# A graph layer on one Trainium2 core: the nodes' own half moves to the middle stage, the permutation gets its own PSUM tile, the order of issue is new

## Chip, core and metric

The kernel runs on one core of a Trainium2 chip. The core has four engines that work in order, each on its own queue: PE (TensorE, matmuls into PSUM), DVE (VectorE), ACT (ScalarE) and POOL (GpSimd). SP (SyncE) issues DMAs. The metric is the device time of one execution in microseconds; the time before is 4208.68 us, the median of 3 runs (4205.73 to 4212.73).

## What is computed

12,500 nodes with 256 features, 200,000 edges (src, dst, weight) sorted by dst. Two graph layers, each added to its input and normalised over the 256 features:

```
feat      = relu(x @ W[o] + b)                       o = 0: self, 1: neighbour; 4 heads of 32
edge_w    = (leaky(att . self)[src] + leaky(att . nei)[dst]) * weight
agg[src] += edge_w * feat_nei[dst]
per head, for self and agg:  (f - mean) * scale * rsqrt(var + 1e-9) + offset
x1  = layernorm(x + concat(self, agg))
msg = relu(concat(x1[src], x1[dst]) @ W_msg + b_msg);   s[dst] += msg
out = layernorm(x1 + layernorm_affine(relu(concat(x1, s) @ W_upd + b_upd)))
```

What the change is about is the self half of the first layer: for each node 128 values (4 heads of 32), centred, divided by the root of their variance, scaled, and added with the offset to the node's x.

## The kernel before

It has three stages.

**First stage, 0 to about 1262 us.** It goes over 112 groups of 14 x 128 edges. In each group it projects 128 nodes twice: the window xw, in which the group's dst values lie (neighbour half), and block xb, the g-th block of 128 nodes (self half, for the 98 groups that have a block). The steps of one group are small functions. `transposes`, `keep`, `project` and `relu` give the features R; `att_mult` and `att_sum` the attention; `mean_sum` and `centre` the centred features F; `part0` to `part3` split the neighbour half into three bf16 parts. The self half then goes through `square` (ACT), `var` (DVE), `root` (ACT), `rstd`, `norm`, `scale` and `put` (DVE) into y, which begins as x plus offset (`offsets`, DVE), and `out_y` stores y in the DRAM table yd.

The edges of a group are sorted by the block of src with one-hot matmuls: `hot` and `hot_b` (DVE) make one-hots, `ranks` (PE) counts, `quarter` (ACT) and `rows` (DVE) round, `begins` (PE), `keep_begins` and `keep_v` (ACT) give the places, `shift` and `reach` (DVE), `steps` (PE), `steps_keep` (ACT), `steps_low` (DVE), `target` (PE) and `index` (DVE) the rows in the log; `place_mm0` to 2 (PE) and `pick0` to 13 (ACT, L667) find each edge's slot; `split`, `hot_r`, `hot_q` and `goods` (DVE) build the operands of `permute` (PE, L696), which puts the edges into order. `extras` (DVE) and `rel_keep` (ACT) read its result. `rel_turn`, `rel_row`, `rel_out` and `rel_in` send the edges' places in the window through DRAM (reld), so that they come back as a row on all partitions (rr); `hot_n` (DVE, L724) compares it; `message0` to 5 (PE, L733) and `evict0` to 5 (ACT, L740) build the messages, and `scatter0` to 3 (POOL, L746) write them into a log in DRAM by indirect DMA.

PSUM tiles of this stage: "fs" (2 of them) is one bank per group; it holds the counts and places, the projection's result and, behind them, the permutation's result. "mp" (3) holds messages, "wp" (2) places, "tp" (1) transposes.

The order of issue is written out by hand: the table AT gives each step a number, step number plus 256 times the group is its place, and all steps of all groups are issued in that order (PE, ACT, DVE and SP keep it exactly). Numbers above 256 mean that a step runs beside the first steps of later groups. Every eighth group the m_ steps (transposes, casts, pair counts) prepare the edge data of eight groups.

**Middle stage, 1262 to 2180 us.** For each of the 98 blocks of nodes the log is read back in five parts: `log_load` (SP), `log_hot` (products by POOL for four parts, by DVE for the fifth; one-hots by DVE, L957), `log_sum` (PE, L965). For batches of up to four blocks (27 batches) `heads_a` to `heads_d` normalise the summed half, `load_y` fetches y from yd, and `stats`, `root`, `rstd`, `offset` and `store_x1` make x1; `proj_t` to `proj_s` project x1 for the second layer. The list `work` is ordered by step, five steps to a block.

**Last stage, 2180 us to the end.** Second layer: gathers by POOL, messages and sums. It is not touched.

Of the kernel before, what the change touches and what calls it, by code (L numbers as in the profile page):

```python
# [11 lines left out]
def _warn_once_fixed(msg, *args, **kwargs):  # L12
# [6 lines left out]
FT = mybir.dt.float32  # L19
# [3 lines left out]
AF = mybir.ActivationFunctionType  # L23
OP = mybir.AluOpType
AX = mybir.AxisListType

P = 128
# [13 lines left out]
    "widen": -271, "hot": -174, "hot_b": -168, "ranks": 42, "quarter": 50, "rows": 89, "begins": 127,  # L41
    "keep_begins": 141, "keep_v": 143, "shift": 201, "reach": 177, "steps": 278, "steps_keep": 303,
# [3 lines left out]
    "split": 381, "hot_r": 405, "goods": 453, "hot_q": 408, "permute": 455, "rel_keep": 503, "extras": 529,  # L46
    "rel_turn": 547, "rel_row": 566, "rel_out": 625, "rel_in": 741, "hot_n": 778, "message0": 830,
# [3 lines left out]
    "project": 180, "relu": 228, "offsets": 376, "att_mult": 309, "mean_sum": 308, "att_sum": 362,  # L51
    "centre": 331, "leaky_n": 392, "part0": 401, "part1": 420, "part2": 561, "part3": 772, "leaky_s": 528,
    "square": 358, "var": 661, "root": 691, "rstd": 725, "norm": 824, "scale": 861, "put": 978, "out_y": 1060,
    "m_load": -1480, "m_cast0": -1441, "m_cast1": -1438, "m_col0": -1038, "m_keep0": -1037, "m_col1": -599,
    "m_keep1": -542, "m_col2": -871, "m_keep2": -834, "m_block": -970, "m_place": -904, "m_high": -277,
    "m_rest": -229, "m_mid": -167, "m_low": -92, "m_win": -504, "m_turn": -771, "m_pairs": -755, "m_mask": -727,
    "m_count": -420,
# [45 lines left out]
def kernel(  # L103
# [45 lines left out]
    yd = dram.tile([ROWS, D], FT, name="yd")  # L149
# [68 lines left out]
    with ExitStack() as l0:  # L218
# [210 lines left out]
        def feat_tasks(g):  # L429
# [28 lines left out]
            def offsets():  # L458
                st["y"] = feat.tile([P, D], FT, name="y", bufs=3)
                nc.vector.tensor_tensor(st["y"], xb[g], ofb, op=OP.add)  # L460

# [58 lines left out]
            def square():  # L520
                st["q"] = feat.tile([P, HD], FT, name="q")
                nc.scalar.activation(st["q"], st["F"][:, 0:HD], AF.Square)

            def var():
                st["v"] = feat.tile([P, H], FT, name="v")
                nc.vector.tensor_reduce(st["v"], st["q"].rearrange("p (h k) -> p h k", h=H), AX.X, OP.add)

            def root():
                nc.scalar.activation(st["v"], st["v"], AF.Sqrt, bias=epsh, scale=1.0 / 32)

            def rstd():
                nc.vector.reciprocal(st["v"], st["v"])

            def norm():
                c = st["F"][:, 0:HD].rearrange("p (h k) -> p h k", h=H)
                nc.vector.tensor_tensor(c, c, st["v"][:, :, None].to_broadcast([P, H, 32]), op=OP.mult)

            def scale():
                c = st["F"][:, 0:HD]
                nc.vector.tensor_tensor(c, c, scb[:, 0:HD], op=OP.mult)  # L540

            def put():
                nc.vector.tensor_tensor(st["y"][:, 0:HD], st["y"][:, 0:HD], st["F"][:, 0:HD], op=OP.add)

            def out_y():
                nc.sync.dma_start(yd[g * P:(g + 1) * P, :], st["y"])
# [3 lines left out]
            return dict(transposes=transposes, keep=keep, project=project, relu=relu, offsets=k(offsets),  # L550
                        att_mult=att_mult, mean_sum=mean_sum, att_sum=att_sum, centre=centre, leaky_n=w(leaky_n),
                        part0=w(part(0)), part1=w(part(1)), part2=w(part(2)), part3=w(part(3)),
                        leaky_s=k(leaky_s), square=k(square), var=k(var), root=k(root), rstd=k(rstd),
                        norm=k(norm), scale=k(scale), put=k(put), out_y=k(out_y))
# [13 lines left out]
        def sort_tasks(g):  # L568
# [124 lines left out]
            def permute():  # L693
                mv = st["mv"].rearrange("p t r m -> p t (r m)")
                for t in range(GT):
                    nc.tensor.matmul(st["sm"][:, 16:16 + 5 * NR], st["qh"][:, :, t], mv[:, t],  # L696
                                     start=(t == 0), stop=(t == GT - 1))
                st["go"] = st["sm"][:, 16:16 + 5 * NR].rearrange("p (r m) -> p r m", m=5)
# [212 lines left out]
    with ExitStack() as bar:  # L911
# [704 lines left out]
```

## Time and profile before

| | us |
|---|---|
| median of 3 runs | 4208.68 |
| the profiled execution | 4196.61 |
| its span, first to last instruction | 4194.8 |
| first stage | about 1262 |
| middle stage | about 918 |
| last stage | about 2015 |

The page gives busy times for each engine over the span; "PEld" is PE's weight load, which overlaps its matmuls. "PEclk" is the clock that the throttle granted PE, 1.00 being full. Rows of groups read: line, engine, operation, output from inputs, shapes, count, then busy us and mean ns of one, then the engine's idle time before them with what ended it. Rows of waits read: who waited, for whom, us in total, times, the longest. Rows of a stretch read: from, to and length in us, then the busy time and instruction count of PE, PEld, DVE, ACT and POOL, the granted clock, the DMA engines' busy share and GB/s. Rows of the timeline read: start and length in us, engine, line, operation, how many, and in brackets the idle time ahead with its cause. Records of neighbouring instructions on one engine overlap a little, so that their mean lengths add up to more than the busy time.

### The profile page before, as it was taken

The page shows a single profiled execution, that of the slowest core. Times are in us where ns is not written, and L with a number is a line of the kernel's source. Part 1 is how long each engine was busy: PE and PEld are TensorE (multiplying, and loading weights), DVE is VectorE, ACT ScalarE, POOL GpSimd, SP SyncE. Part 2 cuts the span into 40 slices and gives each one's busy share as a digit, 9 for nine tenths or more (in the row PEclk, how much of TensorE's full clock was granted, in tenths as well). Part 3 has the DMA queues.
Part 4 walks back from the last instruction along what each step waited for, and adds up shares of the span by engine and source line. Part 5 has one row for each costly group of instructions (what it writes and reads, how often), then busy time and mean ns, then how long its engine had stood idle before and what let it go on. Part 6 is the DMA issues. An engine that isn't in the chain of part 4 may idle for free.

```text
span 4194.8 us, 86344 instructions
## 1 busy us (share of the span) xinstructions
PE 3623.5 (86%) x26432; PEld 3058.0 (73%) x26432; DVE 3206.7 (76%) x9815; ACT 2478.4 (59%) x8632; POOL 2616.8 (62%) x2461
## 2 busy tenths in 40 slices
PE   7889899998889999999988878878888787888876
PEld 6778787777778888888876666666666666666665
DVE  8988989899868888888876666667666666666665
ACT  6998889999881222222235555556565555555555
POOL 2555545555455555555537777777777777777775
PEclk9999999999999999999999999999999999999999
DMA  4776765555556666666656666666666666666664
GB/s 156 242 242 231 237 208 197 191 190 193 173 189 194 185 186 184 181 184 183 187 156 170 171 170 169 170 170 171 171 171 171 172 171 168 172 171 170 171 171 128
DMA packets 457247, 763.84 MB, mean 182 GB/s; under 512 B 75772, under 2 KB 300574, under 8 KB 456782
## 3 DMA queue, kind: packets, MB, share of 16 engines
q1 hardware_dynamic: 326622, 415.17, 34.2%
q0 software_dynamic: 110848, 327.87, 25.6%
q10 hardware_dynamic: 19312, 15.21, 1.1%
q8 instruction: 216, 3.54, 0.4%
q14 instruction: 249, 2.04, 0.2%
HBM read 553.43 MB, written 204.54 MB: 181 GB/s over the span
## 4 chain that ended last, share of the span: by engine, by line
PE 45%; DMA 22%; DVE 16%; ACT 7%; issue 5%; POOL 4%; DVEq 0%; SPq 0%; ACTq 0%; POOLq 0%
PE sum L965 19%; DMA gb<-pd,srcf 19%; PE agg L1363 6%; POOL gb L1285 4%; DVE gb L1344 4%; PE mp L733 4%; ACT gb L1346 3%; PE qp L1322 2%; PE qm L1053 2%; DMA rr<-reld 2%; PE fs L696 2%; PE fs L600 1%; PE fs L467 1%; DMA reld<-rT 1%; DVE oT L724 1%
## 5 line engine op out<-in xcount | busy, mean ns | idle before, releaser
L1285 POOL DMA_INDIRECT gb<-pd,srcf x1563 | 1507.9, 965 | 511.8 <-issue 283.2
L1363 PE MATMUL agg<-gb,o 128*128 128x256 f32 x3126 | 866.9, 400 | 263.8 <-ACT gb L1346 259.2
L1344 DVE TENSOR_TENSOR gb<-qp,gb 128x512 f32<-128x512 f32 x781 | 538.9, 690 | 653.1 <-DMA gb<-pd,srcf 466.7
L746 POOL DMA_INDIRECT log<-m,ix x448 | 631.4, 1409 | 621.8 <-ACT rT L708 264.4
L1346 ACT ACTIVATE gb<-gb 128x512 f32<-128x512 f32 x781 | 491.3, 629 | 790.4 <-DVE gb L1344 786.8
L1363 PEld LDWEIGHTS agg<-gb,o 128*128 128x128 f32 x3126 | 557.0, 192 | 493.5 <-ACT gb L1346 434.3
L965 PE MATMUL sum<-lg,o 128*128 128x256 f32 x3724 | 836.8, 378 | 11.2 <-DMA lg<-log 11.2
L965 PEld LDWEIGHTS sum<-lg,o 128*128 128x128 f32 x3724 | 696.3, 189 | 108.9 <-POOL lg L952 11.4
L957 DVE TENSOR_SCALAR o<-iotap,lg 128x128 f32<-128x128 f32 x1862 | 628.2, 402 | 125.6 <-PE sum L965 115.5
L952 POOL TENSOR_TENSOR lg<-lg 128x512 f32<-128x512 f32 x392 | 412.6, 1065 | 416.4 <-DMA lg<-log 241.3
L1322 PE MATMUL qp<-qh,oT 128*128 128x256 f32 x1563 | 545.1, 371 | 2.4 <-DVE oT L1309 2.4
L667 ACT ACTIVATE junk<-wp,nbig 128x99 bf16<-128x99 f32 x1568 | 529.7, 358 | 5.0 <-PE wp L640 4.5
L733 PE MATMUL mp<-F,oT 128*128 128x132 bf16 x5376 | 411.5, 229 | 5.4 <-DVE lim L826 3.6
L1322 PE MATMUL qp<-ql,oT 128*128 128x256 f32 x1563 | 407.9, 283 | 0.0
L733 PEld LDWEIGHTS <-oT 128*128 128x128 bf16 x5376 | 362.2, 103 | 25.6 <-DVE lim L826 3.8
L667 ACT ACTIVATION_READ_ACCUMULATOR junk<-wp,nbig 128x1 f32 x1568 | 341.2, 218 | 0.0
L1322 PEld LDWEIGHTS qp<-qh,oT 128*128 128x128 f32 x1563 | 299.9, 192 | 20.8 <-DVE oT L1309 2.8
L1322 PEld LDWEIGHTS qp<-ql,oT 128*128 128x128 f32 x1563 | 300.4, 192 | 17.9
L1309 DVE TENSOR_SCALAR oT<-dr,baseP 128x256 fp32r<-128x256 int32 x782 | 289.0, 370 | 11.0 <-DMA dr<-in_dst_dram 11.0
L740 ACT COPY m<-mp 128x396 f32<-128x396 f32 (+1 forms) x672 | 289.4, 448 | 6.2 <-PE mp L733 6.0
L1330 ACT ACTIVATE o<-iotac,rel 128x128 f32<-128x128 f32 x782 | 266.0, 387 | 1.8 <-issue 1.5
L972 ACT COPY S<-sum 128x256 f32<-128x256 f32 x98 | 36.5, 372 | 336.8 <-PE sum L965 336.8
(253 smaller groups left out, 6478.8 us busy)
## 6 DMA issues: line engine op xcount, KB each, us to landing
lg<-log SPq DMA_DIRECT2D x392, 268.0 KB
dr<-in_dst_dram SPq DMA_DIRECT2D x781, 128.0 KB
rr<-reld SPq DMA_DIRECT2D x112, 512.0 KB
log<-zero SPq DMA_DIRECT2D x101, 268.0 KB
gb<-pd,srcf POOLq DMA_INDIRECT x1563
lg<-log SPq DMA_DIRECT2D x98, 201.0 KB
xw<-in_x_dram SPq DMA_DIRECT2D x112, 128.0 KB
xw<-x1d SPq DMA_DIRECT2D x112, 128.0 KB
```

Of the source, the lines that this page charges most:

```text
L667: nc.scalar.activation(small("junk", NBX, BF, p=P), st["w", i][:, k * NBE:k * NBE + NBX], AF.Relu, bias=nbig, accum_out=st["sl"][:, t:t + 1])
L733: nc.tensor.matmul(mp[:, r * (HD + H):(r + 1) * (HD + H)], st["oT"][:, r0 + r], F3[g][:, k], start=(k == 0), stop=(k == 2))
L740: nc.scalar.copy(st["m"][:, r0:r0 + n, 0:HD + H], st.pop(("mp", i))[:, :n * (HD + H)].rearrange("p (r w) -> p r w", r=n))
L746: ins = nc.gpsimd.indirect_dma_start(out=log[:, :], out_offset=bass.IndirectOffsetOnAxis(ap=st["ix"][:, k:k + 1], axis=0), in_=st["m"][:, ...
L952: e.tensor_tensor(t[:, 1, :n, 0:HD].rearrange("p r (h k) -> p r h k", h=H), t[:, 0, :n, 0:HD].rearrange("p r (h k) -> p r h k", h=H), t[:, ...
L957: nc.vector.tensor_scalar(o[:, r], iotap, t[:, 0, r, MW - 2:MW - 1], t[:, 0, r, MW - 1:MW], op0=OP.is_equal, op1=OP.mult)
L965: nc.tensor.matmul(sums[b], o[:, r], t[:, :, r, 0:HD], start=(k == 0 and r == 0), stop=(k == NK - 1 and r == n - 1))
L1285: nc.gpsimd.indirect_dma_start(out=gb[s][:r, i], out_offset=None, in_=pd[:, :], in_offset=bass.IndirectOffsetOnAxis(ap=srci[:r, t:t + 1], ...
L1322: nc.tensor.matmul(qp[:r, i], oT[:, i * P:i * P + r], q, start=(k == 0), stop=(k == 1))
L1344: nc.vector.tensor_tensor(z, qp, z, op=OP.add)
L1346: nc.scalar.activation(z, z, AF.Relu)
L1363: nc.tensor.matmul(agg[g], o[:r, i], z[:r, i], start=(j == 0 and i == 0), stop=lastmm)
```

## The change

- The first stage no longer makes y. `offsets`, `square`, `var`, `root`, `rstd`, `norm`, `scale` and `put` are gone; `out_f` stores the centred self half (128 values) in a table selfd, half as wide as yd was.
- The middle stage's `load_y` loads x and selfd, four steps earlier; y has 4 buffers, not 3. New functions normalise the own half for a batch at once: `own_s` and `own_r` on ACT, `own_b` and `own_c` on DVE, `own_o` (offset) and `own_d` (scale and add) on POOL.
- `permute` writes into a tile of the messages' kind ("mp"), not into the group's bank.
- All numbers of AT are new.

```diff
--- before.py
+++ after.py
@@ -38,23 +38,22 @@
 
 
 AT = {
-    "widen": -271, "hot": -174, "hot_b": -168, "ranks": 42, "quarter": 50, "rows": 89, "begins": 127,
-    "keep_begins": 141, "keep_v": 143, "shift": 201, "reach": 177, "steps": 278, "steps_keep": 303,
-    "steps_low": 367, "target": 390, "index": 479, "place_mm0": 150, "place_mm1": 188, "place_mm2": 248,
-    "pick0": 184, "pick1": 191, "pick2": 197, "pick3": 206, "pick4": 224, "pick5": 234, "pick6": 265,
-    "pick7": 278, "pick8": 296, "pick9": 302, "pick10": 310, "pick11": 315, "pick12": 317, "pick13": 323,
-    "split": 381, "hot_r": 405, "goods": 453, "hot_q": 408, "permute": 455, "rel_keep": 503, "extras": 529,
-    "rel_turn": 547, "rel_row": 566, "rel_out": 625, "rel_in": 741, "hot_n": 778, "message0": 830,
-    "evict0": 845, "message1": 861, "evict1": 886, "message2": 863, "evict2": 929, "message3": 900,
-    "evict3": 930, "message4": 928, "evict4": 985, "message5": 1035, "evict5": 1075, "scatter0": 970,
-    "scatter1": 980, "scatter2": 987, "scatter3": 1096, "load": -167, "transposes": 98, "keep": 116,
-    "project": 180, "relu": 228, "offsets": 376, "att_mult": 309, "mean_sum": 308, "att_sum": 362,
-    "centre": 331, "leaky_n": 392, "part0": 401, "part1": 420, "part2": 561, "part3": 772, "leaky_s": 528,
-    "square": 358, "var": 661, "root": 691, "rstd": 725, "norm": 824, "scale": 861, "put": 978, "out_y": 1060,
-    "m_load": -1480, "m_cast0": -1441, "m_cast1": -1438, "m_col0": -1038, "m_keep0": -1037, "m_col1": -599,
-    "m_keep1": -542, "m_col2": -871, "m_keep2": -834, "m_block": -970, "m_place": -904, "m_high": -277,
-    "m_rest": -229, "m_mid": -167, "m_low": -92, "m_win": -504, "m_turn": -771, "m_pairs": -755, "m_mask": -727,
-    "m_count": -420,
+    "widen": -269, "hot": -161, "hot_b": -113, "ranks": -88, "quarter": -49, "rows": 21, "begins": 26,
+    "keep_begins": 111, "keep_v": 98, "shift": 147, "reach": 192, "steps": 163, "steps_keep": 171,
+    "steps_low": 243, "target": 348, "index": 391, "place_mm0": 112, "place_mm1": 170, "place_mm2": 260,
+    "pick0": 131, "pick1": 137, "pick2": 154, "pick3": 214, "pick4": 218, "pick5": 239, "pick6": 245,
+    "pick7": 306, "pick8": 335, "pick9": 344, "pick10": 351, "pick11": 353, "pick12": 367, "pick13": 369,
+    "split": 417, "hot_r": 417, "goods": 473, "hot_q": 466, "permute": 531, "rel_keep": 600, "extras": 608,
+    "rel_turn": 625, "rel_row": 646, "rel_out": 712, "rel_in": 879, "hot_n": 902, "message0": 905,
+    "evict0": 905, "message1": 922, "evict1": 926, "message2": 980, "evict2": 1025, "message3": 1003,
+    "evict3": 1041, "message4": 1054, "evict4": 1132, "message5": 1131, "evict5": 1141, "scatter0": 930,
+    "scatter1": 1058, "scatter2": 1117, "scatter3": 1153, "load": 67, "transposes": 160, "keep": 163,
+    "project": 186, "relu": 253, "att_mult": 452, "mean_sum": 312, "att_sum": 460, "centre": 507,
+    "leaky_n": 587, "part0": 612, "part1": 651, "part2": 729, "part3": 812, "leaky_s": 865, "out_f": 673,
+    "m_load": -1688, "m_cast0": -1611, "m_cast1": -1401, "m_col0": -1072, "m_keep0": -1020, "m_col1": -491,
+    "m_keep1": -417, "m_col2": -517, "m_keep2": -497, "m_block": -930, "m_place": -843, "m_high": -420,
+    "m_rest": -238, "m_mid": -219, "m_low": -176, "m_win": -71, "m_turn": -824, "m_pairs": -669, "m_mask": -530,
+    "m_count": -417,
 }
 BIG = 4096.0
 MAGIC = 1.5 * 2.0 ** 23
@@ -146,7 +145,7 @@
     reld = dram.tile([NG, P * NR], BF, name="reld")
     x1d = dram.tile([ROWS, D], FT, name="x1d")
     pd = dram.tile([ROWS, D], FT, name="pd")
-    yd = dram.tile([ROWS, D], FT, name="yd")
+    selfd = dram.tile([ROWS, HD], FT, name="selfd")
 
     def bcast_row(ap1d, n):
         return ap1d.rearrange("(o n) -> o n", o=1).to_broadcast([P, n])
@@ -455,10 +454,6 @@
                 nc.scalar.copy(xT[:, a:z].rearrange("p c q -> p (c q)"), st["tp"][:, a * P:z * P])
                 st["xT"] = xT
 
-            def offsets():
-                st["y"] = feat.tile([P, D], FT, name="y", bufs=3)
-                nc.vector.tensor_tensor(st["y"], xb[g], ofb, op=OP.add)
-
             def project():
                 fp = bank[g][:, 0:D] if ww else ps.tile([P, 512], FT, name="fs")[:, 0:D]
                 nc.tensor.matmul(fp[:, lo:hi], ones3, bias3[:, lo:hi], start=True, stop=False)
@@ -517,41 +512,15 @@
                 a = st["a"][:, 0:H]
                 nc.vector.scalar_tensor_tensor(atts[:, g, :], a, 0.2, a, op0=OP.mult, op1=OP.max)
 
-            def square():
...
-            def out_y():
-                nc.sync.dma_start(yd[g * P:(g + 1) * P, :], st["y"])
+            def out_f():
+                nc.sync.dma_start(selfd[g * P:(g + 1) * P, :], st["F"][:, 0:HD])
 
             w = lambda f: f if ww else None
             k = lambda f: f if bb else None
-            return dict(transposes=transposes, keep=keep, project=project, relu=relu, offsets=k(offsets),
+            return dict(transposes=transposes, keep=keep, project=project, relu=relu,
                         att_mult=att_mult, mean_sum=mean_sum, att_sum=att_sum, centre=centre, leaky_n=w(leaky_n),
                         part0=w(part(0)), part1=w(part(1)), part2=w(part(2)), part3=w(part(3)),
-                        leaky_s=k(leaky_s), square=k(square), var=k(var), root=k(root), rstd=k(rstd),
-                        norm=k(norm), scale=k(scale), put=k(put), out_y=k(out_y))
+                        leaky_s=k(leaky_s), out_f=k(out_f))
 
         scatters, zeros = [], []
         zero = dcp.tile([P, RW * MW], FT, name="zero")
@@ -692,10 +661,11 @@
 
             def permute():
                 mv = st["mv"].rearrange("p t r m -> p t (r m)")
+                go = ps.tile([P, 512], FT, name="mp", bufs=3)[:, :5 * NR]
                 for t in range(GT):
-                    nc.tensor.matmul(st["sm"][:, 16:16 + 5 * NR], st["qh"][:, :, t], mv[:, t],
+                    nc.tensor.matmul(go, st["qh"][:, :, t], mv[:, t],
                                      start=(t == 0), stop=(t == GT - 1))
-                st["go"] = st["sm"][:, 16:16 + 5 * NR].rearrange("p (r m) -> p r m", m=5)
+                st["go"] = go.rearrange("p (r m) -> p r m", m=5)
 
             def rel_keep():
                 nc.scalar.copy(small("rs", NR, BF, p=P), st["go"][:, :, 0])
@@ -1064,12 +1034,57 @@
             nc.scalar.activation(t, ys[q][:, i], AF.Identity, bias=nmr[:, b:b + 1], scale=rsd[:, b:b + 1])
             nc.sync.dma_start(x1d[b * P:(b + 1) * P, :], t)
 
-        ys = {}
+        ys, fs = {}, {}
 
         def load_y(q):
             b, n = spans[q]
-            ys[q] = bw.tile([P, BB, D], FT, name="y", bufs=3)
-            nc.sync.dma_start(ys[q][:, :n], yd[b * P:(b + n) * P, :].rearrange("(b p) w -> p b w", p=P))
+            y = ys[q] = bw.tile([P, BB, D], FT, name="y", bufs=4)
+            fs[q] = bw.tile([P, BB, HD], FT, name="fs")
+            m = min(n, N // P - b)
+            if m < n:
+                nc.vector.memset(y[:, m], 0.0)
+                nc.sync.dma_start(y[:N % P, m], x[(b + m) * P:N, :])
+            if m:
+                nc.sync.dma_start(y[:, :m], x[b * P:(b + m) * P, :].rearrange("(b p) w -> p b w", p=P))
+            nc.sync.dma_start(fs[q][:, :n], selfd[b * P:(b + n) * P, :].rearrange("(b p) w -> p b w", p=P))
+
+
+        own = {}
+
+        def own_s(q):
+            b, n = spans[q]
+            own[q] = bw.tile([P, BB, HD], FT, name="oq", bufs=1), bw.tile([P, BB * H], FT, name="ov")
+            nc.scalar.activation(own[q][0][:, :n], fs[q][:, :n], AF.Square)
+
+        def own_b(q):
+            b, n = spans[q]
+            t, v = own[q]
+            nc.vector.tensor_reduce(v[:, :n * H].rearrange("p (b h) -> p b h", h=H),
+                                    t[:, :n].rearrange("p b (h k) -> p b h k", h=H), AX.X, OP.add)
+
+        def own_r(q):
+            b, n = spans[q]
+            v = own[q][1]
+            nc.scalar.activation(v[:, :n * H], v[:, :n * H], AF.Sqrt, bias=epsh, scale=1.0 / 32)
+
+        def own_c(q):
+            b, n = spans[q]
+            v = own.pop(q)[1]
+            F3 = fs[q][:, :n].rearrange("p b (h k) -> p (b h) k", h=H)
+            nc.vector.reciprocal(v[:, :n * H], v[:, :n * H])
+            nc.vector.tensor_tensor(F3, F3, v[:, :n * H, None].to_broadcast([P, n * H, 32]), op=OP.mult)
+
+        def own_o(q):
+            b, n = spans[q]
+            y = ys[q][:, :n]
+            nc.gpsimd.tensor_tensor(y, y, ofb[:, None, :].to_broadcast([P, n, D]), op=OP.add)
+
+        def own_d(q):
+            b, n = spans[q]
+            F = fs.pop(q)[:, :n]
+            nc.gpsimd.tensor_tensor(F, F, scb[:, None, 0:HD].to_broadcast([P, n, HD]), op=OP.mult)
+            y = ys[q][:, :n, 0:HD]
+            nc.gpsimd.tensor_tensor(y, y, F, op=OP.add)
 
         def centre_proj():
 
@@ -1096,7 +1111,10 @@
             for d, f in ((0, heads_a), (1, heads_s), (2, heads_b), (3, heads_r), (4, heads_c), (5, heads_d),
                          (8, stats), (9, root), (10, rstd), (10, offset)):
                 work[t0 + d].append(lambda q=q, f=f: f(q))
-            work[b * NK].append(lambda q=q: load_y(q))
+            t1 = b * NK
+            for d, f in ((-4, load_y), (2, own_s), (3, own_b), (4, own_r), (5, own_c), (1 + n // 2, own_o),
+                         (6 + 2 * (n > 1), own_d)):
+                work[t1 + d].append(lambda q=q, f=f: f(q))
             for i in range(n):
                 for d, f in ((8, proj_t), (9, proj_k), (11, proj_m), (13, proj_s), (13, store_x1)):
                     work[t0 + d + (NK - 1) * i].append(lambda b=b, i=i, f=f: f(b + i))
```

More of the change, by code (lines that the diff above doesn't have):

```diff
@@ L518, in leaky_s @@
                 nc.vector.scalar_tensor_tensor(atts[:, g, :], a, 0.2, a, op0=OP.mult, op1=OP.max)
-            def square():
[L521 to L543, printed above, removed]
-            def out_y():
-                nc.sync.dma_start(yd[g * P:(g + 1) * P, :], st["y"])
+            def out_f():
+                nc.sync.dma_start(selfd[g * P:(g + 1) * P, :], st["F"][:, 0:HD])
             w = lambda f: f if ww else None
             k = lambda f: f if bb else None
-            return dict(transposes=transposes, keep=keep, project=project, relu=relu, offsets=k(offsets),
+            return dict(transposes=transposes, keep=keep, project=project, relu=relu,
                         att_mult=att_mult, mean_sum=mean_sum, att_sum=att_sum, centre=centre, leaky_n=w(leaky_n),
                         part0=w(part(0)), part1=w(part(1)), part2=w(part(2)), part3=w(part(3)),
-                        leaky_s=k(leaky_s), square=k(square), var=k(var), root=k(root), rstd=k(rstd),
-                        norm=k(norm), scale=k(scale), put=k(put), out_y=k(out_y))
+                        leaky_s=k(leaky_s), out_f=k(out_f))
         scatters, zeros = [], []
```

## The prediction

> **What bounds the kernel now.** I read the page first, then the busy times of the three stages, then eight single groups of the first stage, and last the waits there.
>
> The page's sums of busy time name no bound, because they average over three stages. The slices (104.9 us each) show them apart: ACT is at 8 or 9 tenths up to slice 11, at 2 up to slice 20, and at 5 behind that.
>
> ```profile
> PE 3623.5 (86%) x26432; PEld 3058.0 (73%) x26432; DVE 3206.7 (76%) x9815; ACT 2478.4 (59%) x8632; POOL 2616.8 (62%) x2461
> ...
> PE   7889899998889999999988878878888787888876
> ...
> ACT  6998889999881222222235555556565555555555
> ```
>
> Busy time by stage (stretch, length, then PE, PEld, DVE, ACT, POOL, granted clock, DMA share, GB/s):
>
> ```profile
> 60.00:1060.00 1000.00, 897.91 (x11428) 788.79 (x11428) 908.23 (x3064) 898.35 (x4375) 527.58 (x368) 0.96 0.63 214
> 1262.00:2180.00 918.00, 914.85 (x4321) 795.54 (x4322) 788.15 (x2353) 199.66 (x470) 475.10 (x440) 1.00 0.62 181
> 2180.00:4194.00 2014.00, 1608.26 (x8265) 1300.23 (x8263) 1317.06 (x3760) 1185.94 (x2855) 1507.94 (x1563) 0.98 0.62 169
> ```
>
> In the first stage three engines are each at 90% and none is full. In the middle stage PE is full (914.85 of 918) with DVE at 86%. The last stage is not touched. The change takes work from a stage in which three engines hold each other up and gives it to a stage in which PE alone is the bound.
>
> Groups of the first stage, from the projection of one group to that of the next:
>
> ```profile
> 847.02:857.28 10.26, 9.56 (x128) 8.34 (x127) 8.93 (x33) 9.74 (x49) 5.08 (x5) 1.00 0.55 190
> 857.28:870.10 12.82, 11.03 (x127) 9.85 (x125) 12.25 (x38) 10.22 (x51) 6.75 (x4) 0.87 0.52 165
> 870.10:880.55 10.45, 9.34 (x125) 8.18 (x124) 8.94 (x35) 8.54 (x45) 5.10 (x4) 1.00 0.50 179
> 880.55:891.78 11.23, 9.52 (x126) 8.21 (x124) 10.67 (x36) 11.16 (x53) 5.83 (x4) 1.00 0.54 177
> ...
> 901.75:911.47 9.72, 9.20 (x127) 8.13 (x125) 9.15 (x33) 9.49 (x49) 6.14 (x5) 1.00 0.71 235
> 911.47:921.19 9.72, 9.20 (x126) 8.12 (x125) 9.16 (x34) 9.49 (x48) 6.06 (x5) 1.00 0.58 195
> ```
>
> A quiet group takes 9.72 us: PE works 9.20, ACT 9.49, DVE 9.15. The mean group takes 10.87 (46 groups in the 500 us from 560 on). The difference of 1.15 us is made every eight groups, where the tasks that prepare eight groups of edges (the m_ tasks) come on top. In the 12.82 us group DVE is busy for 12.25: it is the bound there, with L393 and L397 (0.97 and 0.96 us) added. PE then starves, and its clock drops.
>
> ```profile
> 862.77 0.82 PE L600 MATMUL fs<-onesb,A 128*99 128x1 bf16 x14 [1.56 <-DVE m L713]
> 863.45 2.64 PE L733 MATMUL mp<-F,oT 128*128 128x132 bf16 x27
> ```
> ```profile
> 860.60:864.02 3.42, 1.86 (x31) 1.71 (x30) 3.42 (x10) 2.12 (x15) 0.00 (x0) 1.00 0.58 195
> 864.04:867.44 3.40, 3.40 (x28) 3.40 (x26) 3.33 (x14) 2.48 (x13) 2.53 (x1) 0.50 0.14 18
> ```
>
> PE lacked 1.56 us of 3.42 and ran the next 3.4 us at half clock; 27 matmuls took 2.64 us there against 1.73 in a quiet group. Every stretch at half clock between 60 and 1250 us that I looked at follows 0.8 to 1.9 us of PE idleness; the 0.53 us of a quiet group never brings one.
>
> The waits from 560 to 1060 us name the largest cause of PE's idle time:
>
> ```profile
> PE fs L600 <- DVE m L713: 36.0, 46, 1.8
> DVE ix L660 <- PE fs L696: 27.4, 46, 1.4
> ```
>
> ranks (L600) of group g+2 takes the PSUM bank in which group g's permutation (L696) lies, and waits until extras (L712, L713) has read it: 0.78 us a group in the mean, 0.53 in a quiet one. DVE's index, ahead of extras, itself waits 0.60 a group for that permutation.
>
> **The change part by part.**
>
> *Removed from each of 98 groups.* DVE loses six instructions (L460 413 ns, L526 279, L532 171, L536 282, L540 279, L543 285: 1.71 us as records). Records overlap; from start to next start the timeline gives 0.33+0.20+0.17+0.20+0.20+0.20 = 1.30. ACT loses L522 (319) and L529 (306), start to next start 0.41. So a quiet group comes to PE 9.20, ACT 9.08, DVE 7.85: PE is the floor, ACT close behind. SP's store shrinks from 128 to 64 KB and can go as soon as the centred half exists, not after put.
>
> *The permutation in a message tile.* PE's instructions stay the same. The wait of ranks for extras goes; next late is index (391), which ranks of g+2 (512-88=424) follows with 33 steps to spare, 1.3 us at 10 us per 256 steps. The new wait is for one of three message tiles: permute (531) needs evict1 of an earlier group, 117 steps before it. Cost between 0 and the 0.53 it replaces; I take 0.1, since evict1 sits so far ahead. Queued behind permute on PE are begins and message4; extras and rel_keep wait for it.
>
> *The new order.* What it brings is not in the trace, so I bound it. Floor: 9.20 for PE or 9.08 for ACT, whichever holds. Ceiling, nothing gained: 9.72 in a quiet group. The nearest row is that of the last groups, which have no own half (three groups, quiet):
>
> ```profile
> 1190.14:1217.37 27.23, 25.83 (x357) 22.42 (x355) 22.61 (x73) 27.05 (x137) 16.13 (x13) 1.00 0.55 189
> ```
>
> 9.08 us a group, PE 8.61, DVE 7.54, ACT 9.02: with DVE relieved, ACT is full and PE idles 0.47. So ACT stands in the way as soon as DVE does not. I take 9.5, in the middle of floor and ceiling. The tightest new pair is hot_n (902) and message0 (905): PE waits there if DVE has no lead. DVE's work from extras to the end of hot_n is 0.37+0.15+0.75 = 1.3 us, PE's between permute and message0 (begins, message4 and 5, target, place_mm0, rel_turn) about 2.75, so 1.4 us are spare. SP: a load (2 x 128 KB) now goes between rel_out and rel_in; rel_row to hot_n grows from 212 to 256 steps (8.7 to 9.5 us at the old and new group), so I cost it at nothing; without that cover it is the 0.9 us that hot_n waited for rr at worst in the last groups. POOL's scatters are four as before and POOL is at 53%: nothing. load to transposes shrinks from 265 to 93 steps, but SP stops only at rel_out ahead of it, so it runs early; a late one would stop PE for a landing, about 2 us.
>
> *The 1.15 us between a quiet and a mean group.* Bounds 0 to 1.15 again. With 1.3 us less on DVE the 12.82 group (DVE 12.25) comes near 10.9, and without its half-clock stretch (1.7 us) near 10. m_pairs and m_mask now lie 139 steps apart. What stays: ACT's m_ work (L339, L360, L366: 11.5 us in 46 groups, 0.25 each) on an engine that is nearly full, and PE's (18 transposes of 0.27, 0.1 each). I take 0.45. Mean group: 9.5+0.45 = 9.95 against 10.87, 0.92 x 98 = 90 us. The 14 groups without own half gain nothing, ACT being full there.
>
> *Ends of the stage.* The last scatter moves from step 1096 to 1153: 57 steps, +2 us.
>
> *Added to the middle stage, per batch of four blocks* (36.8 us: 19 batches in 700 us). DVE: own_b like L993 (676 ns), own_c like L1006 and L1007 (243+692): 1.61 us on 33.1. ACT: 0.63+0.31 on 20% load. POOL: own_d like these two, own_o twice the first:
>
> ```profile
> L1013 POOL TENSOR_TENSOR A<-A,scb 128x512 f32<-128x512 f32 x19 | 29.8, 1568 | 0.0
> ...
> L1015 POOL TENSOR_TENSOR y<-y,A 128x512 f32<-128x512 f32 x19 | 24.1, 1269 | 1.5
> ```
>
> 2.84+3.1 = 6 us on 19.8. All of it lies beside PE's sums. The cover, read off the timeline: the one-hots of a step are done 3.2 to 5.7 us before PE uses them, the products of POOL 12.6 us or more before. DVE takes 1.6 of its 3.2, POOL 6 of its 12.6, behind whose instructions the next products queue; the y load (now 768 KB, not 512; POOL idled 4.9 us for the log after one) adds some 2.5. I take +3 us for the stage (0 to +30); without cover it would be 26 x 1.6 = 42 for DVE alone.
>
> A rule speaks against this part. The trace's nearest pair is L1007 on DVE (692 ns) against L1015 on POOL (1269), the same 128x512: POOL is 1.83 times slower. "GPSIMD Engine Reference", section Elementwise, says to keep such work on the vector engine (1.96 times slower), and its Key points say that the two contend where the vector engine has two SBUF inputs. By the rule the stage would be better with own_o and own_d on DVE; by the rows that would fill DVE (33.1+1.6+3.4 of 36.8).
>
> *Sum* against the profiled execution's own 4196.6: -90+2+3 = -85, 4111.6. The median of the runs is 12.1 above that execution, so 4124.
>
> **The rivals.**
>
> *PE keeps a wait in each group.* The bank's wait returns as one for the message tile, for hot_n or for keep, or ACT's fullness holds PE as in the 9.08 us groups; only DVE's overload goes. 9.72 + 0.75 = 10.47: 0.4 x 98 = 39 us, 4170. For it: ACT's 9.02 of 9.08. This is also the case in which the permutation's move does nothing.
>
> *Slower: DVE's hot_n stops PE each group long enough for the clock.* If PE waits over about 0.9 us at message0, each group has a stretch at half clock: 9.2+0.9+1.7 = 11.8, 0.93 x 98 = +91, 4300. It decides where DVE's spare 1.4 us is gone, because extras comes late. Against it: permute lies 118 steps ahead. "TensorE: Matmul & The Clock Gate", Part 1, tells of a throttle after an idle window of about 3.4 us; by it no group here would be throttled, now or then, and this case would be faster than before (10.1 us a group). The row above shows the drop after 1.56 us, so the row counts.
>
> *The middle stage turns DVE-bound.* If POOL's 6 us lengthen DVE's two-input instructions (L952 on DVE has a median of 551 ns and a maximum of 1404), 4 x 0.85 + 4 x 0.7 = 6.2 us a batch on 34.7 is 40.9: 4 x 23 = 93 us lost, 4214, no change. It decides beyond 2.1 us a batch. Against it: means, not maxima, hold today.
>
> **How the numbers follow.** Forecast 0.66, wait kept 0.21, clock case 0.08, DVE-bound 0.05. 0.2% is 8.4 us, about what a measurement of this kernel can tell from no change. The third case is all slower, the fourth splits over same and slower, and 0.01 of the second is same: faster 0.86, same 0.04, slower 0.10. Range: ACT's 9.08+0.25 = 9.33 and 0.1 of waits give 9.43, 1.44 x 98 = 141 us, 4068, and a little less for the last groups; the upper end takes in the kept wait and 30 us in the middle stage, 4200. The forecast's own range is 4065 to 4160.
>
> **What would show it.** Right: the first stage ends near 1170 us; L600 no longer waits for L713; mean group below 10.1; fewer half-clock stretches; middle stage 918 to 925 us with PE full. Wrong: PE waiting at message0 or permute, clock below 0.95 in the first stage, L965 waiting for DVE or POOL, or a stage-one group above 10.5.

## The result: 1.5% faster, and where it came from

The changed kernel takes 4137.6 us (median of 4 runs, 4134.26 to 4155.56) against 4207.2 us before (4 runs): a ratio of 0.985, 95% interval 0.981 to 0.9889. The forecast was 4124, in a range of 4060 to 4200. The profiled execution has a span of 4135.9 us against 4194.8.

Its page, busy time of each engine and the slices of PE and ACT (103.4 us each):

```profile
PE 3594.4 (87%) x26432; PEld 3015.0 (73%) x26432; DVE 3203.5 (77%) x9309; ACT 2447.4 (59%) x8490; POOL 2623.4 (63%) x2542
...
PE   7999999998989999999988788788877887888876
...
ACT  6888899998942222222235555555556555656555
```

ACT's high slices end one earlier. By the stages (the same columns as before; the middle stage now begins at 1199 us):

```profile
60.00:1060.00 1000.00, 928.00 (x11992) 797.41 (x11991) 858.48 (x2638) 897.56 (x4405) 431.73 (x387) 0.98 0.65 217
1199.20:2110.00 910.80, 908.15 (x4280) 788.55 (x4281) 873.12 (x2412) 215.09 (x504) 606.81 (x520) 1.00 0.65 188
2134.00:4135.00 2001.00, 1594.10 (x8254) 1290.97 (x8254) 1315.38 (x3757) 1178.36 (x2845) 1503.72 (x1557) 0.99 0.62 169
```

PE in the first stage is at 92.8% instead of 89.8%, DVE has fallen from 90.8% to 85.8%. The middle stage is still full on PE, and DVE there has risen from 86% to 96%. That is more than the added instructions. From 1400 to 2100 us DVE is busy 672.1 us instead of 602.7, in a batch of 36.84 us 35.4 instead of 31.7: 3.7 us more, where 1.61 were forecast. The product in heads_c, the same instruction before (L1007) and after (L977), shows where the rest comes from (count, then ns min/median/max):

```profile
L1007 DVE TENSOR_TENSOR A<-A,v x27: 291/692/693, 1283.9 to 2173.8; 128x512 f32<-128x512 f32 x23, 128x128 f32<-128x128 f32 x3, 128x384 f32<-128x384 f32 x1
L977 DVE TENSOR_TENSOR A<-A,v x27: 293/1570/1582, 1223.7 to 2115.0; 128x512 f32<-128x512 f32 x23, 128x128 f32<-128x128 f32 x3, 128x384 f32<-128x384 f32 x1
```

Of the 23 with 128x512 elements none ran beside an elementwise instruction of POOL before; after, 22 do, and take 1290 to 1582 ns, while the one that doesn't takes 693. With the sum in heads_a it is the same: 691 to 692 ns for the 4 alone, 1420 to 1482 for the 19 with POOL beside them. So DVE's instructions with two inputs take about twice as long beside POOL's, and the change puts more of POOL's beside them.

Cut by the starts of the projection's first matmul and of the sums' matmuls, in us:

| | before | after | difference | forecast |
|---|---|---|---|---|
| start to the first projection | 27.7 | 30.8 | +3.1 | |
| first to last projection, 111 groups | 1201.3 | 1134.4 | -66.8 | -90 |
| last projection to the first sum | 33.4 | 33.9 | +0.5 | +2 |
| first to last sum (middle stage) | 906.6 | 910.8 | +4.2 | +3 |
| last sum to the end | 2025.9 | 2025.9 | 0.0 | 0 |
| span | 4194.8 | 4135.9 | -58.9 | -85 |

The mean group fell from 10.88 to 10.27 us (groups 10 to 95); 9.95 was forecast. Half-clock stretches between 60 us and the first sum fell from 26 with 123 us to 10 with 61 us.

Four groups of the changed kernel:

```profile
875.07:884.21 9.14, 9.14 (x124) 8.00 (x125) 8.24 (x26) 9.14 (x47) 4.46 (x5) 1.00 0.69 217
893.85:904.07 10.22, 9.68 (x126) 8.22 (x125) 9.57 (x29) 9.11 (x47) 4.34 (x4) 1.00 0.50 172
904.07:915.29 11.22, 9.94 (x126) 8.35 (x126) 10.91 (x34) 9.63 (x50) 6.10 (x6) 1.00 0.57 199
915.29:924.71 9.42, 9.40 (x124) 8.15 (x125) 8.45 (x29) 9.34 (x48) 3.84 (x5) 1.00 0.61 210
```

In the first of them PE and ACT are both full: that is the floor, 9.14 us, and it is reached. But it is reached seldom; the median group takes 10.09. Waits from 60 to 1060 us, two rows of the kernel before and then the changed one:

```profile
PE fs L600 <- DVE m L713: 76.0, 92, 2.3
...
DVE oT L724 <- DMA rr<-reld: 10.6, 12, 1.7
```
```profile
DVE oT L694 <- DMA rr<-reld: 73.7, 45, 9.0
ACT R L470 <- DVE dw L620: 55.5, 64, 1.7
...
PE mp L703 <- DVE oT L694: 43.2, 30, 8.6
...
PE mp L666 <- DVE mv L654: 7.2, 17, 0.6
```

The wait of ranks for extras (76 us in these 1000 us before) is gone. Two others have taken its place. DVE waits 73.7 us in hot_n (L694) for the row rr, and PE 43.2 us for hot_n at message0 (L703). ACT waits 55.5 us at relu (L470) until DVE's steps_low (L620) has read the same PSUM bank. Before, hot_n waited for rr 10.6 us in the same stretch.

How rr comes to be late is seen on SP's queue (start, length, issue). Before, nothing stands between rel_out and rel_in:

```profile
712.74 0.33 SPq L716 DMA_DIRECT2D reld<-rT  x1
714.36 0.34 SPq L720 DMA_DIRECT2D rr<-reld  x1
```

After, with DVE and PE behind it:

```profile
712.27 0.32 SPq L686 DMA_DIRECT2D reld<-rT  x1
713.77 0.36 SPq L420 DMA_DIRECT2D xw<-in_x_dram  x1
714.23 1.05 SPq L426 DMA_DIRECT2D xb<-in_x_dram  x1
716.02 0.33 SPq L690 DMA_DIRECT2D rr<-reld  x1
```
```profile
720.39 0.75 DVE L694 TENSOR_SCALAR oT<-rr,pcol 128x2048 bf16<-128x2048 bf16 x1 [1.58 <-DMA rr<-reld]
```
```profile
721.20 1.22 PE L703 MATMUL mp<-F,oT 128*128 128x132 bf16 x18 [0.61 <-DVE oT L694]
```

Between rel_out and rel_in stand the two loads of the nodes' rows. Over groups 10 to 95 rel_in follows rel_out by 2.91 us in the mean, against 2.17 before, and the loads' 256 KB are issued ahead of rr's 512 KB on the same queue. When the row has landed is told by the semaphore that hot_n waits for: in the mean of these groups 5.12 us after rel_in's issue, against 4.36 before. Counted from the end of rel_row, which writes rT, the row lands after 8.06 us, against 6.68 before, and DVE is free for hot_n after 7.86, against 8.13. The row used to be 1.45 us ahead of DVE. Its own lateness took 1.38 of that, DVE's earlier arrival 0.27.

### The profile page after: what moved, and what is told of

Read it like the earlier page. It is cut to its first block, busy times and chain, and to the rows that moved or that the text cites. A ratio compares the mean times of both kernels' runs of the same rounds, so it can differ in the third digit from the quotient of the medians.

```text
span 4135.9 us, 85771 instructions
## 1 busy us (share of the span) xinstructions
PE 3594.4 (87%) x26432; PEld 3015.0 (73%) x26432; DVE 3203.5 (77%) x9309; ACT 2447.4 (59%) x8490; POOL 2623.4 (63%) x2542
## 4 chain that ended last, share of the span: by engine, by line
PE 38%; DMA 26%; DVE 14%; ACT 11%; issue 6%; POOL 4%; SPq 1%; DVEq 0%; ACTq 0%; POOLq 0%
DMA gb<-pd,srcf 19%; PE sum L935 19%; DMA rr<-reld 6%; PE agg L1381 6%; DVE gb L1362 4%; POOL gb L1303 4%; ACT gb L1364 3%; ACT junk L636 2%; PE qm L1023 2%; PE qp L1340 2%; PE mp L703 2%; DVE mv L654 1%; ACT m L710 1%; DVE oT L694 1%; DVE A L561 1%
## 5 line engine op out<-in xcount | busy, mean ns | idle before, releaser
L716 POOL DMA_INDIRECT log<-m,ix x448 | 504.4, 1126 | 685.1 <-ACT m L710 452.0
L927 DVE TENSOR_SCALAR o<-iotap,lg 128x128 f32<-128x128 f32 x1862 | 612.1, 397 | 39.5 <-PE sum L935 30.8
L636 ACT ACTIVATE junk<-wp,nbig 128x99 bf16<-128x99 f32 x1568 | 590.9, 402 | 1.9 <-PE wp L609 1.7
L922 POOL TENSOR_TENSOR lg<-lg 128x512 f32<-128x512 f32 x392 | 426.2, 1100 | 230.1 <-DMA lg<-log 133.8
L703 PE MATMUL mp<-F,oT 128*128 128x132 bf16 x5376 | 394.5, 223 | 46.7 <-DVE oT L694 45.2
L636 ACT ACTIVATION_READ_ACCUMULATOR junk<-wp,nbig 128x1 f32 x1568 | 400.9, 256 | 0.0
L703 PEld LDWEIGHTS <-oT 128*128 128x128 bf16 x5376 | 333.4, 99 | 58.5 <-DVE oT L694 51.1
L710 ACT COPY m<-mp 128x396 f32<-128x396 f32 (+1 forms) x672 | 317.5, 488 | 48.5 <-PE mp L703 45.9
```

What stands on the lines that cost most here:

```text
L636: nc.scalar.activation(small("junk", NBX, BF, p=P), st["w", i][:, k * NBE:k * NBE + NBX], AF.Relu, bias=nbig, accum_out=st["sl"][:, t:t + 1])
L703: nc.tensor.matmul(mp[:, r * (HD + H):(r + 1) * (HD + H)], st["oT"][:, r0 + r], F3[g][:, k], start=(k == 0), stop=(k == 2))
L710: nc.scalar.copy(st["m"][:, r0:r0 + n, 0:HD + H], st.pop(("mp", i))[:, :n * (HD + H)].rearrange("p (r w) -> p r w", r=n))
L716: ins = nc.gpsimd.indirect_dma_start(out=log[:, :], out_offset=bass.IndirectOffsetOnAxis(ap=st["ix"][:, k:k + 1], axis=0), in_=st["m"][:, ...
L922: e.tensor_tensor(t[:, 1, :n, 0:HD].rearrange("p r (h k) -> p r h k", h=H), t[:, 0, :n, 0:HD].rearrange("p r (h k) -> p r h k", h=H), t[:, ...
L927: nc.vector.tensor_scalar(o[:, r], iotap, t[:, 0, r, MW - 2:MW - 1], t[:, 0, r, MW - 1:MW], op0=OP.is_equal, op1=OP.mult)
```

## Experiments

The theory at this point: the bank's wait and DVE's load were the cost of the first stage, as forecast, and the rest of the forecast gain went into the late rr. Rivals: DVE's load alone; the bank alone; ACT as the bound, which would hide rr; the new order as the source of the gain.

### One part at a time

Four kernels take the change apart: the own half moved (half), the permutation in a message tile (tile), the new order. The new order can't be had without the tile, because in it ranks of group g+2 is issued ahead of extras of group g.

These four ran on a chip whose last stage was slower (143 GB/s there, against 170), so that the kernel before takes 4594.55 us on it; they are to be compared with that time alone.

**Half alone.**

```diff
 "leaky_s": 528,
-"square": 358, "var": 661, "root": 691, "rstd": 725, "norm": 824, "scale": 861, "put": 978, "out_y": 1060,
+"out_f": 548,
...
+ own_s, own_b, own_r, own_c, own_o, own_d and load_y as in the changed kernel
```

> The order and the permutation's place of before; only the nodes' own half moves to the middle stage (its store at step 548, where SP's queue had the store of y). Theory that DVE's overload in the m_ groups was the first stage's cost: mean group falls from 10.87 to about 10.3, the wait of L600 for extras stays near 0.5 us a group, half-clock time falls by half; 45 to 60 us faster than before. Rival, that ACT and the bank hold the groups and the half only moves work: mean group 10.7 or more, 0 to 15 us faster.

4558.5 against 4594.55: ratio 0.9918 (0.9901 to 0.9934), 36 us faster. Less than the theory's 45 to 60, more than the rival's 15. In its first 1000 us PE still waits for the bank:

```profile
PE fs L570 <- DVE m L683: 49.8, 84, 2.0
```

That is ranks waiting for extras, 0.53 us for each of the 94 groups in the stretch. The quiet group takes 9.66 us (9.72 before), the mean group 10.54, not the 10.3 expected. Half-clock time didn't fall by half either: 116 us, against 123 in the profile of the kernel before, which is from another chip. So DVE's relief pays hardly at all in the quiet groups.

**Tile alone.**

```diff
+go = ps.tile([P, 512], FT, name="mp", bufs=3)[:, :5 * NR]
 for t in range(GT):
-    nc.tensor.matmul(st["sm"][:, 16:16 + 5 * NR], st["qh"][:, :, t], mv[:, t],
+    nc.tensor.matmul(go, st["qh"][:, :, t], mv[:, t],
```

> The kernel before with only the permutation's result in a message tile. Theory (overload of DVE): ranks no longer waits for extras, but DVE stays full in the m_ groups; quiet group 9.5, mean group 10.6 to 10.7, 15 to 30 us faster. Rival (the bank is what holds PE): mean group about 10.2, 60 us or more faster. Third: the wait comes back as one for a message tile, no change.

4543.1: ratio 0.9887 (0.9871 to 0.9904), 51 us faster, between the theory and the rival. The mean group takes 10.61 us, as the theory had it; the quiet group falls to 9.38. In the first 1000 us no engine is full, with DVE close to PE:

```profile
60.00:1060.00 1000.00, 929.41 (x11742) 804.89 (x11741) 926.61 (x3145) 915.84 (x4499) 536.82 (x379) 0.97 0.64 219
```

**Half and tile, old order.**

```diff
 both edits above, AT of before
```

> Own half in the middle stage and permutation in a message tile, order of before. If the new order brings little by itself: within 15 us of the changed kernel (70 us faster than before). If the new order is what makes the two fit: only the sum of the two runs with one part each, or less, 50 us faster or below. If the new order costs (its DMA of the row rr comes later): faster than the changed kernel, 80 us or more faster than before.

4509.9: ratio 0.9809 (0.9783 to 0.9835), 85 us faster. That is the sum of the two (36 and 51) within their intervals, and it is what the third case says: more than the changed kernel's gain. So the new order may cost time. As this chip is slower, the same kernel was also run on another (below).

**Order and tile, own half in the first stage.**

```diff
-"offsets": 376, "square": 358, "var": 661, "root": 691, "rstd": 725, "norm": 824, "scale": 861, "put": 978, "out_y": 1060
+"offsets": 552, "square": 534, "var": 837, "root": 867, "rstd": 901, "norm": 1000, "scale": 1037, "put": 1154, "out_y": 1236
 the rest of AT and permute as in the changed kernel
```

> New order and permutation in a message tile, own half still in the first stage (its eight steps placed behind centre at the distances they had). Theory (DVE's overload): DVE has again 1.3 us more a group, mean group 10.7 or more, within 20 us of before, or slower since the order was laid out without these steps. Rival (order and bank make the gain): 40 us or more faster than before.

4635.4: ratio 1.0092 (1.0065 to 1.0118), 41 us slower than before. The rival that order and tile make the gain falls. How much of the loss is due to the places chosen here for the eight steps was not tried.

**Half and tile, old order, on a chip where the last stage takes 2000 us.**

> Own half in the middle stage and permutation in a message tile, with the order of before, on a chip where the last stage takes its 2000 us, to stand beside the two changed orders: 75 to 90 us faster than before, that is 10 to 20 us faster than the changed kernel. If the gap to the changed kernel was the other chip's: 60 to 70 us faster than before.

4069.8 against 4196.8: ratio 0.9697 (0.9671 to 0.9722), 127 us faster, more than either case expected and twice the gain of the changed kernel, whose 0.9848 (0.9813 to 0.9882) was measured again in another set of runs against 4200.5. Two of its groups and its first 1000 us:

```profile
60.00:1060.00 1000.00, 960.47 (x12766) 845.09 (x12764) 900.06 (x2816) 955.05 (x4702) 536.92 (x413) 0.99 0.67 229
881.25:890.36 9.11, 9.11 (x126) 8.14 (x125) 8.16 (x26) 9.10 (x47) 5.26 (x5) 1.00 0.61 215
890.36:899.46 9.10, 9.10 (x126) 8.14 (x125) 8.31 (x28) 9.10 (x47) 5.16 (x5) 1.00 0.71 239
```

PE at 96%, ACT at 95.5%, the quiet group at its floor of 9.10 and the mean group at 9.67. So the two moves are worth 127 us here, and the new order takes some 63 of them back. Why the same kernel gained 85 us on the first chip (mean group 10.16) was not found; the sizes of the four runs there hold for that chip alone, and how the 127 us divide between half and tile isn't known.

Even with the load where it was, hot_n waits more than the 10.6 us of before:

```profile
DVE oT L695 <- DMA rr<-reld: 43.2, 44, 2.8
```

Here the row is not late: it lands 6.49 us after rel_row, against 6.68 before. But DVE is free for it after 6.49 us, not 8.13. This part of the wait was hidden by DVE's load.

### What the new order costs: the load

**The changed kernel again**, beside the next three:

> The changed kernel again, beside the three that follow on the same chip: 60 to 75 us faster than before; first stage ending near 1199 us, DVE waiting some 75 us for rr in it.

4136.8, 64 us faster than before; hot_n waits 75.0 us for rr.

**The load behind rel_in.**

```diff
-"load": 67
+"load": -106
```

> The changed kernel with the load of the nodes' rows at step -106 instead of 67: on SP's queue it then stands behind rel_in, not between rel_out and rel_in. Theory that this place delays rr: rel_in follows rel_out by 2.1 us again (3.7 in the changed kernel), DVE's wait for rr falls from 74 us in the first 1000 to under 20, PE's wait for hot_n from 43 to under 12, 25 to 45 us faster than the changed kernel. Rival, that ACT is the bound and hides it: waits move to ACT, within 8 us of the changed kernel.

4093.5: 43 us faster than the changed kernel (ratio to before 0.9752, 0.972 to 0.9783). SP's queue:

```profile
714.53 0.33 SPq L686 DMA_DIRECT2D reld<-rT  x1
715.88 0.33 SPq L690 DMA_DIRECT2D rr<-reld  x1
717.25 0.35 SPq L420 DMA_DIRECT2D xw<-in_x_dram  x1
```

and its waits from 60 to 1060 us:

```profile
DVE oT L694 <- DMA rr<-reld: 30.3, 23, 9.1
...
PE mp L703 <- DVE oT L694: 14.9, 10, 8.7
```

The theory's mechanism holds in time and in waits; 30 and 15 us are left where under 20 and 12 were expected. rel_in follows rel_out by 2.07 us in the mean of groups 10 to 95, not 2.91 (the expectation's 3.7 is the one group shown above), and the row lands 6.91 us after rel_row, not 8.06.

**The same place in the old order.** The mirror image, in the kernel with half and tile:

```diff
-"load": -167
+"load": -106
```

> The same kernel with its load at step -106 instead of -167: in this order that puts the load between rel_out and rel_in, as the changed kernel has it. Theory that this place delays rr by the loads' issue and bytes: DVE's wait for rr rises from 36 us in the first 1000 to 70 or more, 20 us or more slower than with the load where it was. Rival, that the delay is the new order's own (hot_n close to message0): within 8 us.

4106.9 against 4069.8: 37 us slower (0.9797, 0.976 to 0.9835, against 0.9697), and hot_n's wait rises from 43.2 to

```profile
DVE oT L695 <- DMA rr<-reld: 96.7, 77, 3.1
```

The row lands 7.72 us after rel_row, not 6.49. So it is the place between rel_out and rel_in that costs, 37 to 43 us in either order, not the neighbourhood of hot_n and message0. PE's loss shows elsewhere there: the first wait of its kind is that of begins for rows, 36.6 us in 1000 against 21.9 with the load where it was.

### What the new order costs: relu behind steps_low

```diff
-"relu": 253
+"relu": 242
```

> The changed kernel with relu at step 242, ahead of steps_low (243), instead of 253. ACT no longer waits at relu until DVE has read the same bank (55 us of its 102 idle us in 1000). Theory that ACT is the bound of a quiet group: 20 to 40 us faster than the changed kernel. Rival, that the late rr is the bound and ACT's wait is slack: within 8 us.

4107.4: 29 us faster than the changed kernel (0.9782, 0.9749 to 0.9816). rr is as late as ever:

```profile
DVE oT L694 <- DMA rr<-reld: 73.8, 48, 9.1
...
PE mp L703 <- DVE oT L694: 40.3, 37, 8.6
```

and the gain comes all the same: ACT, with 897.6 of 1000 us busy in the changed kernel, reaches 933.6:

```profile
60.00:1060.00 1000.00, 943.35 (x12381) 815.66 (x12380) 884.15 (x2729) 933.57 (x4553) 457.38 (x399) 0.99 0.67 223
```

ACT is thus a bound of its own, and its 55 us at relu were no slack. In their place relu waits 15.2 us for the projection, and steps_low 4.5 us for relu.

**Both edits.**

> Both edits. If ACT and rr bound in turn: more than the sum of both gains, 50 us or more faster than the changed kernel. If only rr binds: as with the load alone, 25 to 45 us. If neither: no change.

4073.1: 64 us faster than the changed kernel (0.9697, 0.9666 to 0.9727). Less than the sum of 43 and 29, so the first case falls in its size, but more than either. This brings the new order level with the old one (4069.8): the two edits account in size for what the new order had taken.

### The group of 20 us

Near group 96 one group takes 20.89 us in the changed kernel, with a half-clock stretch of 13.7 us. The theory was that SP stops there for the clearing of the partial block's tile.

```diff
-xb[g] = xin.tile([P, D], FT, name="xb")
-if n < P:
-    nc.vector.memset(xb[g], 0.0)
+xb[g] = xin.tile([P, D], FT, name="xb") if n == P else xlast
...
+xlast = dcp.tile([P, D], FT, name="xlast")
+nc.vector.memset(xlast, 0.0)
```

> Load moved and relu ahead of steps_low, and the last, partial block of nodes loaded into a tile that is cleared once at the start, so that SP's queue doesn't stop at the clearing of it. Theory that this stop holds back rel_in once, near group 96: the group of 20 us takes 10 or 11, the half-clock stretch of 13.7 us behind it goes, 10 to 16 us faster than with the two edits (4073 us). Rival, that the row rr is late there for another cause: no difference.

4072.5, no difference from 4073.1, and a group still takes 19.77 us: this clearing is not the whole cause. The queue shows another:

```profile
955.58 0.33 SPq L686 DMA_DIRECT2D reld<-rT  x1
962.42 0.27 SPq L310 DMA_DIRECT2D mr<-in_src_dram  x1
...
965.41 0.35 SPq L690 DMA_DIRECT2D rr<-reld  x1
```
```profile
962.22 0.45 DVE L308 MEMSET mr<- 107x128 int32 x3
971.15 0.75 DVE L694 TENSOR_SCALAR oT<-rr,pcol 128x2048 bf16<-128x2048 bf16 x1 [8.48 <-DMA rr<-reld]
```

The last load of edge data (m_load) fills its tiles partly, so DVE clears them first, and SP, with rel_in behind that load, waits 6.7 us for it. hot_n then waits 8.48 us. In the changed kernel itself both stops lie between rel_out and rel_in: SP waits 4.7 us at the partial block's load and 1.1 at m_load, rel_in follows rel_out by 10.7 us, and hot_n waits 9.0. Clearing the tiles of m_load early was not tried; that stop is read from the queue, not taken away by a run.

### Which engine for the own half's last steps

```diff
-nc.gpsimd.tensor_tensor(...)   (own_o, own_d)
+nc.vector.tensor_tensor(...)
```

> The changed kernel with own_o and own_d on DVE instead of POOL. By the rows of the middle stage DVE has some 35 of 36.8 us a batch busy already and would take 3.4 us more: PE waits for one-hots, the middle stage grows by 26 x 1.5 = 40 us (20 to 60). Rival, by the skill's rule that such work belongs on the vector engine and that POOL contends with it: DVE's other instructions get shorter, the middle stage stays within 8 us.

4221.1, slower than before (1.0068, 1.0048 to 1.0088). Its middle stage, 999.1 us against 910.8, and PE's wait there (1260 to 2000 us):

```profile
1188.50:2187.60 999.10, 943.59 (x4279) 806.78 (x4280) 945.39 (x2490) 212.28 (x504) 524.00 (x439) 0.97 0.58 171
```
```profile
PE sum L935 <- DVE o L927: 39.8, 18, 3.6
```

88 us, twice the 40 expected: besides DVE's own 3.4 us a batch (the three instructions take 1.47, 0.76 and 1.42 us), PE's waits bring 58 us at half clock into a stage that had none. The rival's sign came in part: the product in heads_c is back at a median of 693 ns, but DVE's product in log_hot, still beside POOL's, rose from 805 to 986 ns in the mean. The rule of the Trainium skill that the prediction weighed ("GPSIMD Engine Reference", section Elementwise: such work belongs on the vector engine) did not hold here, where that engine is at 96%.

## Why the prediction was right, and where it was not

- **The quiet group.** Its floor was given as 9.20 for PE or 9.08 for ACT: measured 9.14, both full. The 9.5 taken was too high for the quiet group itself (9.14 and 9.42 in the groups shown).
- **The bank as what PE waits for in a quiet group, 0.53.** Held: with the half alone the quiet group takes 9.66, with the tile alone 9.38, with both 9.10.
- **The new wait for a message tile, 0.1.** Held: the waits at permute in the changed kernel are for goods, 7.2 us in 1000, not for a tile.
- **The surplus of the mean group, 0.45.** This term was mis-sized: 10.27 less some 9.3 is about 1. With half and tile in the old order it is 0.57 (9.67 less 9.10), near the forecast.
- **"a load (2 x 128 KB) now goes between rel_out and rel_in ... so I cost it at nothing"**. This step failed. The place was seen, but taken as covered, since 256 steps instead of 212 lie between rel_row and hot_n. Steps are no time: from the end of rel_row to the start of hot_n pass 8.63 us, against 8.27 before, not 9.5 against 8.7. That is 0.36 us more, for a row that lands 1.38 us later. The cost is 43 us. The bound of 0.9 us for a single wait was too small too: hot_n waits up to 9.0 us, and in the kernel before it had waited 6.7 once, in the last group.
- **relu behind steps_low** was missing from the sum: 29 us. In these traces ACT's read of the bank waits for DVE's where DVE's is issued first (55.5 us in 1000), and ACT was already named as nearly full.
- **Middle stage, +3.** Measured +4.2, but the number came by luck. DVE took 3.7 us more a batch, not 1.61, because its two-input instructions got longer beside POOL. That the 33.1 us assumed for DVE were too many (602.7 us over 19 batches are 31.7) made up for some of it. The cover was spent further than forecast: one-hots that were 3.2 us or more ahead of PE are 0.06 us ahead at the tightest place (median 0.6 to 0.7 there), not 1.6. It held by little.
- **The rivals.** The kept wait came, at hot_n (43.2 us in 1000), but it didn't hold the quiet group at 9.72, and the mean group is 10.27, not 10.47. The clock case rests on a half-clock stretch behind each wait over 0.9 us. That is not so: PE waited for hot_n at message0 in 30 of 97 groups, in 21 of them for over 0.9 us. The waits of 0.94 to 1.79 us brought no half clock; four of 1.93 to 2.73 and the one of 8.6 us did. The third rival's mechanism came, DVE's two-input instructions beside POOL, at a lower price: 35.4 us of 36.8 a batch, not 40.9. The run with own_o and own_d on DVE shows that 3.4 us more are too many.
- **The signs.** Of those for right, three came: L600's wait is gone, half-clock stretches are fewer, and the middle stage is short and full on PE. Two did not: the first stage ends at 1199 us, not near 1170, and the mean group is 10.27, not below 10.1. Of those for wrong, PE's wait at message0 came.
- **Sums.** 4 x 23 is 92, not 93. 212 steps are 8.7 us only at 10.5 us a group; at the mean group of 10.87 they are 9.0.

The total came out near the forecast by luck, because two errors in it met: the half and the tile are worth more than the 85 us that I gave to the whole (127), and I let the order pass at almost no cost (it took 63).

## What to carry to other kernels

Where three engines hold each other up, take the row of a quiet group for the floor and ask of every step moved on a DMA queue what now waits behind it: a load slipped between a store and the read that depends on it cost 40 us out of 4137 here. Ask by how much the data will land later, and how much earlier its reader will come; steps in an order of issue answer neither. When work moves to POOL, look for DVE instructions with two inputs that will run beside it. Change work and order in separate runs: together they showed 1.5%, and the work alone was worth 3%.

## What was not expected of the hardware

DVE's two-input instructions on 128x512 f32 took 691 to 694 ns alone and 1290 to 1582 in heads_a and heads_c beside an elementwise instruction of POOL.

PE's clock stood at half for 13.7 us round one idle stretch of 8.6 us: from 3.1 us into it to 8.1 us behind it. Shorter stretches of 3.4 or 6.8 us at half follow 0.8 to 2.7 us of idleness in the 3.4 us before them, but no single length divides the waits: 1.56 us ahead of ranks brought one in the kernel before, 1.79 us ahead of message0 none in the changed kernel.

ACT's accumulating step (L636) has a mean record of 402 ns in the changed kernel against 358 before, while from the start of one to the start of the next, where two follow each other, it takes 328 ns in the mean against 322: the record's length is no measure of what ACT spends on it.

On one chip the kernel before took 9% longer (4594.55 us against 4207.2). In the four profiles from that chip the time from the last sum to the end is 2408 to 2416 us, against 2026; with half and tile the DMA engines moved 143 GB/s in the last stage there, 170 for the changed kernel on another chip.
